# Five early W2 blocks by id ahead of the full W2, and b2's rows spread by GpSimd

## The chip, the cores and the metric

The kernel runs on one core of one Trainium2 chip. The metric is the device time of one execution in microseconds, as the median of several. One execution was also taken by the hardware profiler; it has a span, from the first to the last instruction of the program, and an own time, which holds a little work around the span.

## What is computed

For each of 128 batches there is a block x of 128 tokens by 512 channels and an id between 0 and 8, which picks one of ten languages (W1 512x128, b1, W2 128x512, b2, gamma, beta). Everything is float32.

```python
w1, w2 = W1[ids], W2[ids]
h = relu(einsum('bsh,bha->bsa', x, w1) + b1[ids][:, None, :])
r = x + einsum('bsa,bah->bsh', h, w2) + b2[ids][:, None, :]
normed = (r - mean(r)) * rsqrt(var(r) + 1e-5)
return x + normed * gamma[ids][:, None, :] + beta[ids][:, None, :]
```

## The kernel before

A batch is a tile of 128 tokens by 512 channels. For each one TensorE turns x by four transposes (`transpose_x`, L271), ScalarE copies the result out of PSUM (`copy_xT`, L275), TensorE makes the first product with W1 in four steps (`down`, L294), ScalarE applies relu with b1 (`relu`, L302), and TensorE makes the second product with W2 (`up`, L311). b2 gets into the sum in one of three ways, chosen by batch: TensorE adds it by a small matmul in front of the second product (`b2_by_matmul`, L310), VectorE adds it to the product (`b2_by_vector`, L321), or GpSimd adds it to x beforehand (`add_b2`, L281). VectorE adds x and sums the row (`residual`, L328), ScalarE squares and sums (`square`, L351), and the square root and some short steps give 1/std. VectorE applies mean and gamma (`scale`, L394) and 1/std, and adds it to x + beta (`finish`, L403), which GpSimd has made beforehand in an output buffer (`add_beta`, L288). Two batches share one output buffer and one store (`store`, L407).

The engines work on different batches at one time, and the order on each engine, the SP queue included, is the order of the calls (`keep` chains each instruction to the one before it on its engine). The main loop issues, per turn, the transposes of one batch, the first product of the batch before it, and the second product of the batch two behind.

Before the loop stands an opening written out by hand. It loads the rows of beta, gamma and b2 once (30 rows) and splits them into bf16 parts. Each row that the adds read must stand on all 128 partitions. `spread` does this for one row by a matmul (L229) and a copy on ScalarE (L232); `shuffle_rows` does it for one row by a stream shuffle on VectorE (L247) out of a tile that holds the rows four times (`four_copies`). Rows 0 to 9 are beta, 10 to 19 gamma, 20 to 29 b2. An add takes its row by the id from the whole tile (`beta_b`, `gamma_b`, `b2_b`), so it waits until all ten rows are there. `spin` runs matmuls on ones, whose results nobody reads.

All loads but three small ones go through SP's queue, and each load waits until the eighth before it has landed. x comes by groups of four batches in four buffers (`load_part` for the first twenty batches, `load_x` later). W1 comes in two ways: for the first 17 batches one block of 256 KB by the batch's id into one of seven buffers (`load_first`, L161), and as a whole by four loads of 640 KB (`load_w1`, L103), out of which ScalarE copies one block per batch from batch 17 on (`stage_w1`, L262). W2 comes as a whole, in two loads: three languages, then seven (`load_w2`, L165); the second products read it by the id, so each of them waits for both loads. The order in SP's queue in the opening is this:

```python
load_w2(0, 3); load_first(0); load_first(1); load_part(2, 4); load_first(2); load_first(3)
load_w2(3, L); load_part(4, 6); load_first(4); load_first(5); load_part(6, 8); load_first(6) ...
```

GpSimd starts with some constants and an affine select for the identity, then waits for beta's rows. There are eight output buffers of two batches each.

Of the kernel before, what the change touches and what calls it, by code (L numbers as in the profile page):

```python
# [20 lines left out]
EARLY = 17  # L21
LATE = 17
U = 2


@with_exitstack
def cond_resid_kernel(ctx: ExitStack, tc: tile.TileContext, x, itok, W1, b1, W2, b2, gamma, beta, out):
# [18 lines left out]
    def keep(ins):  # L46

        engine = ins.ins.engine
        if engine in last:
            tc.add_manual_dep(ins.ins, last[engine], behind, reason="kept order")  # L50
        last[engine] = ins.ins.name
        return ins
# [1 line left out]
    const = ctx.enter_context(tc.tile_pool(name="const", bufs=1))  # L54
    xp = ctx.enter_context(tc.tile_pool(name="xp", bufs=4))
    rp = ctx.enter_context(tc.tile_pool(name="rp", bufs=4))
    op = ctx.enter_context(tc.tile_pool(name="op", bufs=8))
    tp = ctx.enter_context(tc.tile_pool(name="tp", bufs=2))
    wp = ctx.enter_context(tc.tile_pool(name="wp", bufs=7))
    st = ctx.enter_context(tc.tile_pool(name="st", bufs=6))  # L60
# [25 lines left out]
    def load_part(lo, hi, engine=nc.sync):  # L86
        dst = xs[lo // G][:, lo % G : lo % G + hi - lo, :]
        keep(engine.dma_start(out=dst, in_=x[lo:hi].rearrange("b s h -> s b h")))  # L88

    warm = const.tile([P, 1], FP, name="warm")  # L90
    keep(nc.vector.memset(warm, 1.0))

# [2 lines left out]
    keep(nc.sync.dma_start(out=rows[L : 2 * L, :], in_=gamma))  # L95
    keep(nc.scalar.dma_start(out=rows[2 * L : 3 * L, :], in_=b2))
    load_part(0, 2)
    keep(nc.scalar.dma_start(out=b1r, in_=b1))
    keep(nc.scalar.activation(warm, warm, AF.Abs_reciprocal_sqrt))

    def load_w1(k):
        keep(
            nc.sync.dma_start(out=w1[:, :, k, :], in_=W1[:, k * P : (k + 1) * P, :].rearrange("l p a -> p l a"))  # L103
        )
# [35 lines left out]
    def lid(b, engine):  # L140
        g = b // G
        if (g, engine) not in lids:
            loads, vals = nc.values_load_multi_w_load_instructions(  # L143
                lang[0:1, g * G : (g + 1) * G],
                engines=[engine],
                min_val=0,
                max_val=L - 1,
                skip_runtime_bounds_check_because="clamped on the chip to 0..L-1 above",
            )
            for ins in loads:  # L150
                keep(ins)
            lids[g, engine] = vals
        return lids[g, engine][b % G]
# [4 lines left out]
    def load_first(b):  # L158
        w1s[b] = wp.tile([P, KC, A], FP, tag="w1s", name=f"w1s_{b}")
        src = W1[bass.ds(lid(b, ET.SP), 1)].rearrange("o (p k) a -> p (o k a)", k=KC)  # L160
        keep(nc.sync.dma_start(out=w1s[b].rearrange("p k a -> p (k a)"), in_=src))  # L161

    def load_w2(lo, hi):
        dst = w2[:, lo * H : hi * H].rearrange("p (l h) -> p l h", l=hi - lo)
        keep(nc.sync.dma_start(out=dst, in_=W2[lo:hi].rearrange("l a h -> a l h")))  # L165

    load_w2(0, 3)
    load_first(0)
    load_first(1)
    load_part(2, 4)  # L170
    load_first(2)
    load_first(3)
    load_w2(3, L)
    xs[1] = xp.tile([P, G, H], FP, tag="x", name="x_1")
    load_part(4, 6)
    load_first(4)
    load_first(5)
    load_part(6, 8)
    load_first(6)
    load_first(7)  # L180
    xs[2] = xp.tile([P, G, H], FP, tag="x", name="x_2")
    load_part(8, 10)
    load_first(8)
    load_first(9)
    load_part(10, 12)
    load_first(10)
    load_first(11)
    xs[3] = xp.tile([P, G, H], FP, tag="x", name="x_3")
    load_part(12, 14)
    load_first(12)  # L190
    load_w1(0)
    load_first(13)
    load_part(14, 16)
    load_first(14)
    load_w1(1)
    load_first(15)
    xs[4] = xp.tile([P, G, H], FP, tag="x", name="x_4")
    load_part(16, 18)
    load_w1(2)
    load_w1(3)  # L200
    load_first(16)
    load_part(18, 20)
# [17 lines left out]

    beta_b = const.tile([P, L * H], FP, name="beta_b")
    gamma_b = const.tile([P, L * H], FP, name="gamma_b")
    b2_b = const.tile([P, L * H], FP, name="b2_b")

    def spread(r, copier):
        t = (beta_b, gamma_b, b2_b)[r // L]
        row = p_y.tile([P, H], FP, tag="y", name=f"row_{r}")
        pick_r = pick[:, r : r + 1].to_broadcast([96, P])
        keep(nc.tensor.matmul(row, lhsT=pick_r, rhs=parts[:96, :], start=True, stop=True))  # L229
        dst = t[:, r % L * H : (r % L + 1) * H]  # L230
        if copier is nc.scalar:
            keep(nc.scalar.copy(dst, row))  # L232
        else:
            keep(nc.vector.tensor_copy(dst, row))

    fours = {}

# [6 lines left out]
    def shuffle_rows(lo, hi):  # L244
        for r in range(lo, hi):
            t = (beta_b, gamma_b, b2_b)[r // L]
            keep(nc.vector.stream_shuffle(t[:, r % L * H : (r % L + 1) * H], fours[0], [r] * 32))  # L247
# [3 lines left out]


    def b2_by_matmul(b):
        return b in (0, 1) or b >= B - 2

    def b2_by_vector(b):
        return b in (2, 3, 9, 13, 17, 21) or 24 <= b < B - 8 and (b % 16 in (1, 6, 11) or b % 32 == 30)

    def stage_w1(b):
        w1s[b] = wp.tile([P, KC, A], FP, tag="w1s", name=f"w1s_{b}")  # L260
# [43 lines left out]
    def up(b):  # L304
        v = lid(b, ET.PE)
        ys[b] = p_y.tile([P, H], FP, tag="y", name=f"py_{b}")
        m = b2_by_matmul(b)
        if m:
            pick_b = pick[:, bass.ds(v + 2 * L, 1)].to_broadcast([96, P])
            keep(nc.tensor.matmul(ys[b], lhsT=pick_b, rhs=parts[:96, :], start=True, stop=False))  # L310
        keep(nc.tensor.matmul(ys[b], lhsT=hT[b], rhs=w2[:, bass.ds(v * H, H)], start=not m, stop=True))  # L311
        del hT[b]

    def col(tiles, b):
# [210 lines left out]
    def spin(n, width):  # L525
        idle = p_s.tile([P, H], FP, tag="s", name="idle")
        for _ in range(n):
            keep(
                nc.tensor.matmul(
                    idle[:, :width], lhsT=ones, rhs=ones[:, 0:1].to_broadcast([P, width]), start=True, stop=True  # L530
                )
            )
# [6 lines left out]

    spin(7, H)  # L540
    four_copies()
    spread(10, nc.scalar)
    spin(1, H)
    x_turn(0)
    transpose_b1()
    spread(11, nc.scalar)
    for n in (0, G):
        lid(n, ET.PE)
    shuffle_rows(0, 10)
    x_turn(1)  # L550
    spread(12, nc.scalar)
    spread(13, nc.scalar)
    down(0)
    relu(0)
    spread(14, nc.scalar)
    x_turn(2)
    spread(15, nc.scalar)
    down(1)
    relu(1)
    spread(16, nc.scalar)  # L560
    spread(17, nc.scalar)
    x_turn(3)
    down(2)
    relu(2)
    spread(18, nc.scalar)
    spread(19, nc.scalar)
    add_beta(0)
    add_beta(1)
    spread(20, nc.scalar)
    spread(21, nc.scalar)  # L570
    down(3)
    relu(3)
    spread(22, nc.scalar)
    add_beta(2)
    add_beta(3)
    shuffle_rows(23, 30)
    up(0)
    up(1)
    x_turn(4)

    turned = 5
    for i in range(3, B - 6):
        b = i - U - 1
        if b == 8 or b > 12 and b % G == 2 and b // G + 3 < NG:
            load_x(5 if b == 8 else b // G + 3)
        up_to = i
        if b <= E:
            if turned <= up_to and on(turned):
                transpose_x(turned)
            add_b2(b + 2)  # L590
            if 4 <= b + 2 <= E:
                add_beta(b + 2)
        for n in range(turned, min(B, up_to) + 1):
            if on(n) and (n > turned or b > E):
                transpose_x(n)
            down(n - 1)
            if on(n):
                copy_xT(n)
            relu(n - 1)
            if on(n + 1) and n + 1 >= FIRST:  # L600
                stage_w1(n + 1)
        turned = max(turned, min(B, up_to) + 1)
        if i - U >= 2 and on(i - U):
            up(i - U)

        g, half = divmod(b, 2)
        p = g - 1
        mine, old = 0 <= p < B // 2, 0 <= p - 1 < B // 2
        if half == 0:
            if on(b):  # L610
                vector_b2(b)
                residual(b)
                square(b)
            if mine:
                scale(2 * p)
                rstd(p, 1)
            if old:
                finish(2 * p - 1)
                store(p - 1)
        else:  # L620
            if on(b):
                vector_b2(b)
            if mine:
                rstd(p, 2)
            if on(b):
                residual(b)
                square(b)
            if mine:
                rstd(p, 3)
                scale(2 * p + 1)  # L630
            if mine:
                finish(2 * p)
        if 0 <= g and b <= E and half == 1:
            scalar_means(g)
            deviation(g)

        for n, engine in ((turned + 2, ET.Activation), (i - U + 3, ET.PE), (b + 1, ET.DVE), (b + 6, ET.Pool)):
            if on(n):
                lid(n, engine)
# [189 lines left out]
```

## Time and profile before

| | us |
|---|---|
| median of 3 runs | 303.18 |
| all runs | 303.14 to 303.38 |
| profiled execution, own time | 303.08 |
| its span | 301.3 |

| engine | busy us | share of the span |
|---|---|---|
| PE (TensorE) | 293.5 | 97% |
| DVE (VectorE) | 294.0 | 98% |
| ACT (ScalarE) | 278.5 | 92% |
| POOL (GpSimd) | 281.0 | 93% |

The granted clock is full over the whole span. The transfers move 78.11 MB. In timeline rows the first figure is the start in us from the span's start, the second the duration in us; SP rows give the time that the issue took on the queue, not the transfer's. PE shows a float32 matmul as two records, so a first product has eight and a second product two. The last figure of a row of DMA issues is the time from issue to landing in us.

### The profile page before, as it was taken

Reading aid. Unit: us, or ns where it says so; the run is one execution under the profiler, and the core shown is the slowest. Engines: PE = TensorE matmul, PEld = TensorE weight load, DVE = VectorE, ACT = ScalarE, POOL = GpSimd, SP = SyncE. Lnnn points to the kernel's source line nnn. Section 1 sums busy time; section 2 is a strip of 40 time slices with the busy share of each in tenths; the row PEclk is TensorE's granted clock in tenths of the full one; section 3 lists DMA queues with packets and bytes.
Section 4 is the critical chain, followed back from the end, with each engine's and each line's share of the span. In section 5 each row is a group of like instructions: output and inputs, shape, how many; then the busy total and the mean of one; then the engine's idle time right before and its main releaser. Section 6 shows DMA issues by size and latency. Waiting matters only on the chain.

```text
span 301.3 us, 7022 instructions
## 1 busy us (share of the span) xinstructions
PE 293.5 (97%) x1827; PEld 219.1 (73%) x1827; DVE 294.0 (98%) x785; ACT 278.5 (92%) x770; POOL 281.0 (93%) x236
## 2 busy tenths in 40 slices
PE   7899999999999999999999999999999999999993
PEld 3758787777777777777777777777777777777761
DVE  6989999999999999999999999999999999999996
ACT  5868789999999999999999999999999999999983
POOL 1299998999999999999999999999999999999982
PEclk9999999999999999999999999999999999999999
DMA  6999999996667776766687666668765767782826
GB/s 234 377 390 367 346 321 396 405 337 209 234 229 256 280 235 197 252 242 233 240 281 250 209 209 246 257 231 281 263 204 196 254 232 253 278 271 79 280 89 228
DMA packets 45353, 78.11 MB, mean 259 GB/s; under 512 B 2137, under 2 KB 9316, under 8 KB 45314
## 3 DMA queue, kind: packets, MB, share of 16 engines
q1 hardware_dynamic: 45254, 77.62, 74.9%
q8 instruction: 15, 0.25, 0.3%
q14 instruction: 24, 0.20, 0.2%
q10 hardware_dynamic: 60, 0.05, 0.1%
HBM read 44.11 MB, written 33.55 MB: 258 GB/s over the span
## 4 chain that ended last, share of the span: by engine, by line
PE 87%; DVE 5%; DMA 3%; issue 2%; SPq 1%; POOL 0%; DVEq 0%; POOLq 0%
PE ph L294 35%; PE py L311 35%; PE pxT L271 18%; DMA w<-in_L_cond_W_dram 3%; DVE py L328 1%; DVE o L488 1%; DVE py L394 1%; SPq L161 1%; DVE n L494 0%; SPq L143 0%; DVE rstd_of L370 0%; SPq L88 0%; DVEq L824 0%; DVE part_of L367 0%; DVE shift L434 0%
## 5 line engine op out<-in xcount | busy, mean ns | idle before, releaser
L288 POOL TENSOR_TENSOR o<-x,beta_b 128x512 f32<-128x512 f32 x121 | 158.4, 1331 | 12.8 <-DVE beta_b L247 11.6
L294 PE MATMUL ph<-xT,w1s 128*128 128x128 f32 x1024 | 135.4, 275 | 0.1
L311 PE MATMUL py<-w,hT 128*128 x256 | 131.5, 595 | 0.6 <-DMA w<-in_L_cond_W_dram 0.6
L294 PEld LDWEIGHTS ph<-xT,w1s 128*128 128x128 f32 x1024 | 124.9, 192 | 1.8 <-issue 0.8
L281 POOL TENSOR_TENSOR r<-x,b_b 128x512 f32<-128x512 f32 x92 | 122.7, 1334 | 0.0
L271 PEld LDWEIGHTS pxT<-ident,x 128*128 128x128 f32 x512 | 65.8, 149 | 66.3 <-issue 49.9
L394 DVE SCALAR_TENSOR_TENSOR py<-py,nmean,gamma_b 128x512 f32<-128x512 f32 x124 | 93.2, 752 | 0.0
L403 DVE SCALAR_TENSOR_TENSOR o<-py,rstd,o 128x512 f32<-128x512 f32 x116 | 86.5, 745 | 0.0
L351 ACT ACTIVATE sq<-py,sum 128x512 f32<-128x512 f32 x124 | 85.8, 692 | 0.2 <-DVE rstd L370 0.2
L275 ACT COPY xT<-pxT 128x512 f32<-128x512 f32 x128 | 74.7, 584 | 5.9 <-PE pxT L271 5.8
L271 PE MATMUL pxT<-ident,x 128*128 128x128 f32 x512 | 77.6, 274 | 0.9 <-ACT gamma_b L232 0.7
L328 DVE SCALAR_TENSOR_TENSOR py<-py,r 128x512 f32<-128x512 f32 x97 | 66.7, 688 | 0.1
L262 ACT COPY w1s<-w 128x512 f32 x108 | 66.2, 613 | 0.0
L302 ACT ACTIVATE hT<-ph,b1T 128x128 f32<-128x128 f32 x128 | 46.9, 367 | 8.6 <-PE ph L294 4.0
L311 PEld LDWEIGHTS py<-w,hT 128*128 128x128 f32 x256 | 39.0, 192 | 2.2 <-DMA w<-in_L_cond_W_dram 1.1
L351 ACT ACTIVATION_READ_ACCUMULATOR sq<-py,sum 128x1 f32 x124 | 25.1, 203 | 0.0
L328 DVE SCALAR_TENSOR_TENSOR py<-py,x 128x512 f32<-128x512 f32 x31 | 21.7, 699 | 0.8 <-PE py L311 0.3
L321 DVE TENSOR_TENSOR py<-py,b_b 128x512 f32<-128x512 f32 x27 | 18.6, 689 | 0.8 <-ACT xT L275 0.6
L361 ACT ACTIVATE root<-ssq,eps 128x2 f32<-128x2 f32 x62 | 16.4, 265 | 0.0
L328 DVE DVE_READ_ACCUMULATOR py<-py,r 128x1 f32 x97 | 13.4, 138 | 0.0
L342 ACT ACTIVATE nmean<-sum 128x2 f32<-128x2 f32 x61 | 12.1, 199 | 0.0
L370 DVE SCALAR_TENSOR_TENSOR rstd<-part,root 128x2 f32<-128x2 f32 x62 | 9.2, 149 | 0.0
(73 smaller groups left out, 104.5 us busy)
## 6 DMA issues: line engine op xcount, KB each, us to landing
out_dram<-o SPq DMA_DIRECT2D x62, 512.0 KB, 3.5
x<-in_x_dram SPq DMA_DIRECT2D x27, 1024.0 KB, 6.5
x<-in_x_dram SPq DMA_DIRECT2D x10, 512.0 KB, 6.0
w1s<-in_L_cond_W_dram SPq DMA_DIRECT2D x20, 256.0 KB, 7.7
w<-in_L_cond_W_dram SPq DMA_DIRECT2D x4, 640.0 KB, 8.4
w<-in_L_cond_W_dram SPq DMA_DIRECT2D x1, 1792.0 KB, 10.2
w<-in_L_cond_W_dram SPq DMA_DIRECT2D x1, 768.0 KB, 5.2
out_dram<-o SPq DMA_DIRECT2D x4, 128.0 KB, 1.7
```

The costliest lines, as they stand in the source:

```text
L262: keep(nc.scalar.copy(w1s[b].rearrange("p k a -> p (k a)"), src))
L271: keep(nc.tensor.transpose(pxs[b][:, k, :], cols, ident))
L275: keep(nc.scalar.copy(xT[b], pxs.pop(b)))
L281: keep(nc.gpsimd.tensor_tensor(rs[b], xb(b), b2_b[:, bass.ds(v * H, H)], ALU.add))
L288: keep(nc.gpsimd.tensor_tensor(os[g][:, j, :], xb(b), beta_b[:, bass.ds(v * H, H)], ALU.add))
L294: nc.tensor.matmul(phs[b], lhsT=w1s[b][:, k, :], rhs=xT[b][:, k, :], start=(k == 0), stop=(k == KC - 1))
L302: keep(nc.scalar.activation(hT[b], phs.pop(b), AF.Relu, bias=b1T[:, bass.ds(lid(b, ET.Activation), 1)]))
L311: keep(nc.tensor.matmul(ys[b], lhsT=hT[b], rhs=w2[:, bass.ds(v * H, H)], start=not m, stop=True))
L328: nc.vector.scalar_tensor_tensor(ys[b], ys[b], 1.0, r, ALU.mult, ALU.add, accum_out=col(sums, b))
L351: nc.scalar.activation(sq, ys[b], AF.Square, bias=col(sums, b), scale=-float(H), accum_out=col(ssqs, b))
L394: nc.vector.scalar_tensor_tensor(ys[b], ys[b], col(nmeans, b), gamma_b[:, bass.ds(v * H, H)], ALU.add, ALU.mult)
L403: nc.vector.scalar_tensor_tensor(o, ys[b], rstds[g][:, j : j + 1], o, ALU.mult, ALU.add)
```

## The change

W2 of batches 0 to 4 is also loaded by id, one block of 256 KB each, into three output buffers (`early_w2`, `load_early`), and their second products read those blocks. The full W2 comes in one load behind the loads of x and W1 for the first eight batches. The ten rows of b2 are loaded once more, as one row of 5120 values on one partition, and GpSimd spreads them over all partitions in two broadcasts of 2560 columns; the b2 rows no longer go through matmuls and shuffles. The built program has, on GpSimd, a switch of its code library in front of the broadcasts and one back behind them, in front of the first add of beta. Output buffers go from eight to nine. Of the twenty rows of beta and gamma eight go by matmul and copy, twelve by shuffle. b2 goes by matmul also for batches 4 and 7, and by VectorE for 2, 6, 9, 17, 19 of the first 24 (before: 2, 3, 9, 13, 17, 21); the rest stays with GpSimd. In the opening the second product of batch 0 comes behind the first product of batch 2. In the queue, x of batches 2 to 9 comes batch by batch, x of batches 16 and 17 ahead of W1 of batch 14, and the loads of the full W1 behind it. The load of x for batches 20 to 23 is issued two turns sooner.

```diff
+SOON = 5
-    op = ctx.enter_context(tc.tile_pool(name="op", bufs=8))
+    op = ctx.enter_context(tc.tile_pool(name="op", bufs=9))
...
     load_part(0, 2)
+    keep(nc.scalar.dma_start(out=b2_b[0:1, :], in_=b2.rearrange("(o l) h -> o (l h)", o=1)))
     keep(nc.scalar.dma_start(out=b1r, in_=b1))
...
+    def early_w2(b):
+        if b // 2 not in soon:
+            soon[b // 2] = op.tile([P, 2, H], FP, tag="o", name=f"soon_{b // 2}")
+        return soon[b // 2][:, b % 2, :]
+
+    def load_early(b):
+        src = W2[bass.ds(lid(b, ET.SP), 1)].rearrange("o a h -> a (o h)")
+        keep(nc.sync.dma_start(out=early_w2(b), in_=src))
...
-    load_w2(0, 3)
     load_first(0)
     load_first(1)
-    load_part(2, 4)
     load_first(2)
+    load_part(2, 3)
     load_first(3)
-    load_w2(3, L)
+    load_early(0)
+    load_part(3, 4)
+    load_early(1)
+    load_first(4)
     xs[1] = xp.tile([P, G, H], FP, tag="x", name="x_1")
-    load_part(4, 6)
-    load_first(4)
+    load_part(4, 5)
+    load_early(2)
+    load_early(3)
     load_first(5)
-    load_part(6, 8)
+    load_early(4)
     load_first(6)
     load_first(7)
+    load_part(5, 6)
+    load_part(6, 7)
+    load_part(7, 8)
+    load_w2(0, 10)
...
     load_part(12, 14)
-    load_first(12)
-    load_w1(0)
+    load_part(14, 16)
     load_first(13)
-    load_part(14, 16)
-    load_first(14)
-    load_w1(1)
-    load_first(15)
     xs[4] = xp.tile([P, G, H], FP, tag="x", name="x_4")
     load_part(16, 18)
+    load_first(14)
+    load_w1(0)
+    load_w1(1)
     load_w1(2)
+    load_first(15)
     load_w1(3)
     load_first(16)
     load_part(18, 20)
...
+    for half in range(2):
+        cols = slice(half * (L // 2) * H, (half + 1) * (L // 2) * H)
+        keep(nc.gpsimd.partition_broadcast(b2_b[:, cols], b2_b[0:1, cols]))
...
-        return b in (0, 1) or b >= B - 2
+        return b in (0, 1, 4, 7) or b >= B - 2
...
-        return b in (2, 3, 9, 13, 17, 21) or 24 <= b < B - 8 and ...
+        return b in (2, 6, 9, 17, 19) or 24 <= b < B - 8 and ...
...
-        keep(nc.tensor.matmul(ys[b], lhsT=hT[b], rhs=w2[:, bass.ds(v * H, H)], start=not m, stop=True))
+        rhs = early_w2(b) if b < SOON else w2[:, bass.ds(v * H, H)]
+        keep(nc.tensor.matmul(ys[b], lhsT=hT[b], rhs=rhs, start=not m, stop=True))
...
-        if b == 8 or b > 12 and b % G == 2 and b // G + 3 < NG:
-            load_x(5 if b == 8 else b // G + 3)
+        if b == 6 or b > 12 and b % G == 2 and b // G + 3 < NG:
+            load_x(5 if b == 6 else b // G + 3)
```

More of the change, by code (lines that the diff above doesn't have):

```diff
@@ L88, in load_part @@
         keep(engine.dma_start(out=dst, in_=x[lo:hi].rearrange("b s h -> s b h")))
+    b2_b = const.tile([P, L * H], FP, name="b2_b")
     warm = const.tile([P, 1], FP, name="warm")
@@ L161, in load_first @@
         keep(nc.sync.dma_start(out=w1s[b].rearrange("p k a -> p (k a)"), in_=src))
+    soon = {}
+    def early_w2(b):
[5 more added lines that the diff above has]
+        keep(nc.sync.dma_start(out=early_w2(b), in_=src))
     def load_w2(lo, hi):
@@ L165, in load_w2 @@
         keep(nc.sync.dma_start(out=dst, in_=W2[lo:hi].rearrange("l a h -> a l h")))
-    load_w2(0, 3)
     load_first(0)
     load_first(1)
-    load_part(2, 4)
     load_first(2)
+    load_part(2, 3)
     load_first(3)
-    load_w2(3, L)
+    load_early(0)
+    load_part(3, 4)
+    load_early(1)
+    load_first(4)
     xs[1] = xp.tile([P, G, H], FP, tag="x", name="x_1")
-    load_part(4, 6)
-    load_first(4)
+    load_part(4, 5)
+    load_early(2)
+    load_early(3)
     load_first(5)
-    load_part(6, 8)
+    load_early(4)
     load_first(6)
     load_first(7)
+    load_part(5, 6)
+    load_part(6, 7)
+    load_part(7, 8)
+    load_w2(0, 10)
     xs[2] = xp.tile([P, G, H], FP, tag="x", name="x_2")
-    load_part(8, 10)
+    load_part(8, 9)
+    load_part(9, 10)
     load_first(8)
@@ L187, in cond_resid_kernel @@
     load_first(11)
+    load_first(12)
     xs[3] = xp.tile([P, G, H], FP, tag="x", name="x_3")
     load_part(12, 14)
-    load_first(12)
-    load_w1(0)
+    load_part(14, 16)
     load_first(13)
-    load_part(14, 16)
-    load_first(14)
-    load_w1(1)
-    load_first(15)
     xs[4] = xp.tile([P, G, H], FP, tag="x", name="x_4")
     load_part(16, 18)
+    load_first(14)
+    load_w1(0)
+    load_w1(1)
     load_w1(2)
+    load_first(15)
     load_w1(3)
@@ L222, in cond_resid_kernel @@
     gamma_b = const.tile([P, L * H], FP, name="gamma_b")
-    b2_b = const.tile([P, L * H], FP, name="b2_b")
     def spread(r, copier):
@@ L253, in b2_by_matmul @@
     def b2_by_matmul(b):
-        return b in (0, 1) or b >= B - 2
+        return b in (0, 1, 4, 7) or b >= B - 2
     def b2_by_vector(b):
-        return b in (2, 3, 9, 13, 17, 21) or 24 <= b < B - 8 and (b % 16 in (1, 6, 11) or b % 32 == 30)
+        return b in (2, 6, 9, 17, 19) or 24 <= b < B - 8 and (b % 16 in (1, 6, 11) or b % 32 == 30)
     def stage_w1(b):
@@ L541, in cond_resid_kernel @@
     four_copies()
-    spread(10, nc.scalar)
-    spin(1, H)
+    spread(17, nc.scalar)
+    shuffle_rows(3, 4)
     x_turn(0)
     transpose_b1()
[L546 to L549, printed above, removed]
+    lid(0, ET.PE)
+    lid(G, ET.PE)
     x_turn(1)
-    spread(12, nc.scalar)
-    spread(13, nc.scalar)
+    shuffle_rows(0, 1)
+    spin(1, H)
+    shuffle_rows(10, 11)
+    shuffle_rows(6, 7)
+    shuffle_rows(16, 17)
+    spread(1, nc.scalar)
     down(0)
     relu(0)
-    spread(14, nc.scalar)
+    shuffle_rows(5, 6)
     x_turn(2)
-    spread(15, nc.scalar)
     down(1)
     relu(1)
-    spread(16, nc.scalar)
-    spread(17, nc.scalar)
+    shuffle_rows(14, 15)
+    shuffle_rows(4, 5)
+    spread(9, nc.scalar)
     x_turn(3)
@@ L564, in cond_resid_kernel @@
     relu(2)
-    spread(18, nc.scalar)
-    spread(19, nc.scalar)
+    up(0)
+    shuffle_rows(2, 3)
+    spread(11, nc.scalar)
+    spread(8, nc.scalar)
+    spread(15, nc.scalar)
+    shuffle_rows(19, 20)
+    shuffle_rows(7, 8)
     add_beta(0)
-    add_beta(1)
-    spread(20, nc.scalar)
-    spread(21, nc.scalar)
     down(3)
     relu(3)
-    spread(22, nc.scalar)
+    add_beta(1)
+    spread(13, nc.scalar)
     add_beta(2)
     add_beta(3)
-    shuffle_rows(23, 30)
-    up(0)
+    x_turn(4)
+    shuffle_rows(18, 19)
     up(1)
-    x_turn(4)
+    spread(12, nc.scalar)
     turned = 5
```

## The prediction

> **What bounds the kernel now.** I read the page first (shares, then the chain), then PE's rows, and then the queue of loads, because the change is made in the first 50 us.
>
> ```profile
> PE 293.5 (97%) x1827; PEld 219.1 (73%) x1827; DVE 294.0 (98%) x785; ACT 278.5 (92%) x770; POOL 281.0 (93%) x236
> PE 87%; DVE 5%; DMA 3%; issue 2%; SPq 1%; POOL 0%; DVEq 0%; POOLq 0%
> ```
>
> All four engines are nearly full, but the chain that ended last is PE's. Its order of time begins with a load, and from there PE's rows follow each other without a gap:
>
> ```profile
> 6.22 10.17 DMA w<-in_L_cond_W_dram
> ...
> 23.53 1.02 PE L311 MATMUL py<-w,hT 128*128 x2
> ...
> 25.75 1.02 PE L311 MATMUL py<-w,hT 128*128 x2
> ```
>
> The second part of the full W2 is issued at 6.22 and lands at 16.39; batch 0's second product starts behind it. 23.53 and 25.75 are the second products of batches 4 and 5: 2.22 us a batch, PE's own work. So the time is the moment at which PE reaches its steady pace, plus a fixed rest. Whatever delays PE before about batch 17 is paid once, in full; whatever lets it start sooner is gained only if no later operand is late.
>
> The operands come through one queue. Four stretches of the trace (length, then busy time of PE, PEld, DVE, ACT, POOL, then clock, DMA share, GB/s):
>
> ```profile
> 4.00:16.40 12.40, 10.28 (x66) 7.57 (x65) 11.37 (x35) 10.32 (x23) 3.30 (x3) 1.00 1.03 379
> 16.40:28.00 11.60, 11.57 (x66) 8.30 (x67) 10.43 (x29) 8.11 (x23) 11.60 (x11) 1.00 1.05 386
> 28.00:48.00 20.00, 20.00 (x129) 15.69 (x128) 19.82 (x51) 16.21 (x47) 18.83 (x16) 1.00 1.11 340
> 48.00:100.00 52.00, 52.00 (x332) 39.30 (x332) 51.94 (x138) 50.80 (x142) 52.00 (x43) 1.00 0.81 287
> ```
>
> The DMA share is over 1 up to 48 us and 0.81 behind it. In the opening the queue has no room: a byte put in front of a load delays it by the byte's own time.
>
> **The queue, in blocks.** I count in blocks of 256 KB (one batch of x, one W1 of one language, one W2 of one language) in the order of issue. Issue rows and, below each, the last figure of its DMA row (us to landing):
>
> ```profile
> 3.75 0.91 SPq L161 DMA_DIRECT2D w1s<-in_L_cond_W_dram  x2
> w1s<-in_L_cond_W_dram SPq DMA_DIRECT2D x1, 256.0 KB, 4.1
> ...
> 16.52 1.68 SPq L161 DMA_DIRECT2D w1s<-in_L_cond_W_dram  x2
> w1s<-in_L_cond_W_dram SPq DMA_DIRECT2D x1, 256.0 KB, 8.5
> ...
> 37.63 2.82 SPq L161 DMA_DIRECT2D w1s<-in_L_cond_W_dram  x1
> w1s<-in_L_cond_W_dram SPq DMA_DIRECT2D x1, 256.0 KB, 7.1
> ```
>
> Batch 0's W1 is the 6th block (two of x, three of W2 before it) and lands at 3.75 + 4.1 = 7.85. The end of W2 is the 18th, at 16.39: 0.71 us a block. Batch 8's W1 is the 29th, at 16.52 + 8.5 = 25.0: 0.78 a block. Batch 16's W1 is the 55th, at 37.63 + 7.1 = 44.7; the four loads of the full W1 (10 blocks) lie between, the last as block 54, at about 44.0. At 386 GB/s a block takes 0.68 us.
>
> **What the change puts in the queue.** The full W2 (10 blocks) stays, and five blocks (W2 of batches 0 to 4 by id) are added in front of it. W2 now ends as block 31 (8 of x, 8 of W1, 5 + 10 of W2), the full W1 as block 59, batch 16's W1 as block 60. One more cost: the 3 blocks of W2 that filled the queue while SP waited for the ids are gone from there. Batch 0's W1 is still issued at 3.75, with two blocks in front of it whose load was issued at 1.52 and landed 3.4 later:
>
> ```profile
> 1.52 0.41 SPq L88 DMA_DIRECT2D x<-in_x_dram  x1
> x<-in_x_dram SPq DMA_DIRECT2D x1, 512.0 KB, 3.4
> ```
>
> 3.4 less two blocks (1.4) is a delay of 2.0, so block 3 lands at 3.75 + 2.0 + 0.7 = 6.4, where a queue without a hole would have it at 4.9 + 0.7 = 5.6. The hole is worth 0 to 0.8 us; I take 0.7.
>
> W2 ends at 25.0 + 2 x 0.68 + 0.7 = **27.1** (26.4 without the hole). Batch 5's second product is the first that needs it, and it stood at 25.75: PE is 0.7 to 1.3 us later than before, whatever it gained earlier. Eight smaller blocks are in flight behind W2, so the queue does not run dry while SP waits for W2 to land before it issues batch 12's W1.
>
> Then batch 16's W1 and the full W1. Their readers stood here:
>
> ```profile
> 47.03 1.06 PE L294 MATMUL ph<-xT,w1s 128*128 128x128 f32 x8
> ...
> 46.20 0.61 ACT L262 COPY w1s<-w 128x512 f32 x1
> ```
>
> Batch 16's W1 lands 5 x 0.68 + 0.7 = 4.1 us later, at 48.8, and its product stood at 47.03: +1.8. The full W1 ends at 44.0 + 4.1 = 48.1, and ScalarE's first copy out of it stood at 46.20: +1.9, with the square of batch 13 and the copy of batch 17's x queued behind it on ScalarE; PE waits for that copy. These waits overlap the one at batch 5 and do not add to it: the largest counts, with some 0.2 for the coupling of the two. **Sum: +2.0 us**, bounds +1.1 (no hole) and +2.8 (a second hole as large).
>
> **What is gained and hidden.** Each of these costs or brings nothing, because PE stands waiting for W2 until 27.1 or for W1 until 48.8. If that cover were gone they would count.
>
> ```profile
> 13.50 1.03 PE L229 MATMUL row<-parts,pick 96*128 96x512 bf16 x4
> 16.43 1.12 PE L311 MATMUL py<-w,hT 128*128 x2 [0.58 <-DMA w<-in_L_cond_W_dram]
> 10.04 0.72 PE L271 MATMUL pxT<-ident,x 128*128 128x128 f32 x4 [0.71 <-ACT gamma_b L232]
> 1.70 0.35 ACTq L98 DMA_DIRECT2D b1r<-in_L_cond_b_dram  x1
> L247 DVE STREAM_SHUFFLE b_b<-four x7: 791/795/801, 12.9 to 16.8; 128x512 f32<-128x512 f32 x7
> ```
>
> - Spreads by matmul go from 13 to 8: (1.03 - 0.38) / 3 = 0.22 each, so 1.1 us off PE, and five copies off ScalarE. b2 by matmul for batches 4 and 7: +0.22 each.
> - The waits of 0.58 and 0.71 go. Batch 0's second product can start when its own W2 block is there (block 8, near 10 us). PE alone would reach batch 5 at 25.75 - 1.1 + 0.2 - 1.3 + 0.3 = 23.9, and then waits some 3 us.
> - The load of the b2 row on ScalarE's queue delays its table load and the split rows by 0.3.
> - Shuffles on VectorE go from 17 to 12 at (16.8 - 12.9) / 6 = 0.65: 3.3 us off its opening. b2 on VectorE goes from six of the first 24 batches to five. VectorE follows PE, so neither is seen.
> - The first x of group 4 moves in front of three W1 loads on SP and waits for batch 3's readers, done by then. Loading x 20 to 23 is issued one store sooner.
> - Output buffers: three of nine hold early W2 at first; the tenth pair (batch 18) waits for the first store where the ninth (batch 16) waited 1.17. GpSimd has that much in hand (below).
>
> **GpSimd.** It idles to 13.10 and then adds without a pause, 4.98 / 4 = 1.24 us each:
>
> ```profile
> 0.89 0.20 POOL masks.py:197 MEMSET ident<- 128x128 f32 x1
> 1.03 0.10 POOL L111 MEMSET eps<- 128x1 f32 x1
> 1.17 0.29 POOL masks.py:199 TENSOR_SCALAR_AFFINE_SELECT ident<-ident 128x128 f32<-128x128 f32 x1
> 13.10 4.98 POOL L288 TENSOR_TENSOR o<-x,beta_b 128x512 f32<-128x512 f32 x4 [11.64 <-DVE beta_b L247]
> masks.py:199 POOLq MODIFY_POOL_CONFIG  x2: 11/11/11, 1.1 to 1.1; - x2
> ```
>
> Added: two broadcasts of 128x2560, and a switch of GpSimd's code before them and back before the first add. No row shows a broadcast. The add (1.24 for 512 columns) gives 6.2 us each; the select less a memset of one column, (0.29 - 0.10) / 127 a column, gives 3.8; the memset alone, (0.20 - 0.10) / 127, gives 2.0. I take 3, between the last two: it writes as the memset does, and reads one row. A switch costs nothing in the one row that has it (0.01 us, the select follows at once). So the adds could begin between 1.5 + 4.0 = 5.5 and 1.5 + 12.4 = 13.9, and beta's rows hold them to 13.1 anyway (shuffles end near 13).
>
> How late may they be? b2 of batch 5 is the 7th add (four of beta, b2 of 3, beta of 4): 8.7 us after the start. VectorE wants it when batch 5's product ends, 27.1 + 1.0 = 28.1. So up to a start at **19.4** nothing is lost; each us beyond costs one, since later on 25 of 32 batches have both adds, 57 x 1.24 / 32 = 2.2 us a batch, which cannot catch up. Later there is more in hand:
>
> ```profile
> 68.53 1.28 POOL L281 TENSOR_TENSOR r<-x,b_b 128x512 f32<-128x512 f32 x1
> 73.16 0.70 DVE L328 SCALAR_TENSOR_TENSOR py<-py,r 128x512 f32<-128x512 f32 x1
> ```
>
> Batch 26 is among the tightest: b2 ready at 69.81, used at 73.16, and GpSimd has one add less by then.
>
> The Trainium skill speaks against this part: GPSIMD Engine Reference, 2.1 Instruction dispatch, says the first call to a freshly loaded kernel pays about 6 us for loading code, with no instruction that shows it. No run here shows such a first call; the select's row shows none. By the page two switches put the first add at 1.5 + 6 + 6 + 6 = 19.5, on the edge of the cover.
>
> **Rivals.**
> 1. *GpSimd begins too late* (chance 0.20). If the switches take long, or the broadcast has the add's pace, the first add comes at 21 to 23. Price: 1.6 to 3.6 more, **307.7**. It decides from 19.4 on. For it: two switches to code that this kernel never called; against it: the 0.01 us of the row. The page just named gives this case with broadcasts over 3 us.
> 2. *W2 lands in time* (0.12, faster). If blocks land at 0.65 us instead of 0.71 to 0.78, and those behind W2 at 0.70, W2 ends at 6.4 + 28 x 0.65 = 24.6 and batch 16's W1 at 24.6 + 29 x 0.70 = 44.9; PE's own 23.9 is then covered up to 24.6: 25.75 - 24.6 = 1.2 us gained, **301.9**. It decides where W2 ends before 25.7 and batch 16's W1 before 47.0. Against it: 379 to 386 GB/s with the share over 1 in both stretches. The Trainium skill (DMA: Bandwidth & Descriptors, Specifications) names a ceiling of 435 GB/s, an estimated 0.60 us a block, and would give this case; the rows stay 11% under it.
> 3. *No change* (0.08). The queue's own stops hide the blocks: from block 18 to 29 it took 25.0 - 16.39 = 8.6 us where 11 x 0.68 is 7.5. If that stop of 1.1 falls elsewhere, and no hole opens, 2.0 - 1.1 - 0.7 = +0.2 is left: **303.3**. It decides where batch 16's W1 lands by 47.3.
>
> **How the numbers follow.** The profiled execution took 303.08 with a span of 301.3; the median of three is 303.18. 303.1 + 2.0 = **305.1** (0.60 for this case). The range reaches down to the no-change case and up to 1's middle: **303.2 to 308.2**; the forecast's own bounds are 304.2 to 305.9. Within 0.2% (0.6 us, about what a measurement can tell) is rival 3: same 0.08; faster 0.12; slower 0.60 + 0.20 = 0.80.
>
> **What would show it.** Right: the chain of waits begins with the load of W2 ending at 26.4 to 27.2; PE waits about 3 us before batch 5's second product; ScalarE's first copy out of W1 and batch 16's first product wait for loads near 48; then 2.2 us a batch to the same tail. Wrong: PE without a wait at batch 5, W2 before 25.7, or VectorE waiting for GpSimd's sums past batch 5.

## The result, and the profile after

The changed kernel takes 311.91 us in the median (four runs, 311.05 to 313.71), the kernel before 303.28 beside it: a ratio of 1.030 with an interval of 1.028 to 1.032, slower by 8.6 us. The forecast was 305.1 with a range to 308.2; the sign was right, the size was not. The profiled execution is the longest of the four, 313.71 with a span of 311.9, and is compared with before's own profiled execution (303.08, 301.3): 10.6 us more.

The page after: engine shares, the chain that ended last, and the granted clock in 40 slices of 7.8 us.

```profile
PE 296.8 (95%) x1824; PEld 222.1 (71%) x1824; DVE 290.6 (93%) x774; ACT 276.7 (89%) x765; POOL 285.2 (91%) x237
...
PEclk9897599999999999999999999999999999999999
...
PE 88%; DVE 5%; issue 3%; POOL 2%; ACT 1%; DMA 1%; ACTq 0%; DVEq 0%; POOLq 0%
```

Read by shares, little has happened: every busy time is within a few us of before's. What is new is a clock of 0.8, 0.7 and 0.5 in the second, fourth and fifth slice (a 9 stands for 90% or more), where it was full, and the chain, which has no long DMA piece any more but one of POOL. GpSimd's timeline says why (start, duration, then in brackets the idle time before):

```profile
1.41 0.29 POOL masks.py:199 TENSOR_SCALAR_AFFINE_SELECT ident<-ident 128x128 f32<-128x128 f32 x1 [0.29 <-POOL eps L114]
8.42 5.48 POOL L259 PARTITION_BROADCAST b_b<-b_b  x2 [6.73 <-issue]
24.77 4.91 POOL L313 TENSOR_TENSOR o<-x,beta_b 128x512 f32<-128x512 f32 x4 [10.87 <-issue]
29.65 1.25 POOL L306 TENSOR_TENSOR r<-x,b_b 128x512 f32<-128x512 f32 x1
```

The two broadcasts take 5.48 together. Around them GpSimd stands idle for 6.73 and 10.87 us, both "issue": no semaphore is late. The row of b2 had landed at 4.55, beta's last row was written by 16.5. The first add starts at 24.77 where it stood at 13.10 before. The load of the full W2, issued at 15.72, has fifteen of its sixteen parts landed by 27.16 and the last at 28.71 (by the updates of its semaphore in the trace), so W2 is not what comes last. The chain of waits around PE's stop:

```profile
22.33 0.91 PE ph L319 x8
23.23 0.02 issue
23.26 0.38 ACT hT L327
23.64 1.13 issue
24.77 4.70 POOL o L313 x4
...
29.85 1.05 POOL r L306
...
30.93 0.07 DVE py L354
...
32.28 0.76 DVE o L429
33.04 0.04 issue
33.09 2.08 PE py L337 x2
```

The fifth add is b2 of batch 3 (29.65 to 30.90). VectorE's sum of batch 3 waits for it, `finish` of batch 0 stands behind that sum on VectorE (32.28), and only `finish` gives back the PSUM buffer that batch 5's second product needs. That product starts at 33.09; before it stood at 25.75: 7.3 us. The rest of the 10.6 follows at once. PE's rows behind it:

```profile
33.09 2.08 PE L337 MATMUL py<-w,hT 128*128 x2 [7.42 <-DVE o L429]
34.95 1.06 PE L296 MATMUL pxT<-ident,x 128*128 128x128 f32 x4
35.81 1.92 PE L319 MATMUL ph<-xT,w1s 128*128 128x128 f32 x8
37.52 1.30 PE L337 MATMUL py<-w,hT 128*128 x2
...
40.24 1.02 PE L337 MATMUL py<-w,hT 128*128 x2
```

and four stretches of 4 us (length, busy time of PE, PEld, DVE, ACT, POOL, then granted clock, DMA share, GB/s):

```profile
24.00:28.00 4.00, 1.66 (x13) 1.33 (x11) 0.00 (x0) 0.00 (x0) 3.23 (x3) 0.98 1.05 387
28.00:32.00 4.00, 0.00 (x0) 0.00 (x0) 1.07 (x4) 0.28 (x1) 4.00 (x4) 0.50 1.05 388
32.00:36.00 4.00, 2.91 (x7) 1.78 (x8) 3.81 (x12) 2.36 (x8) 4.00 (x5) 0.50 1.04 383
36.00:40.00 4.00, 4.00 (x23) 3.39 (x22) 2.49 (x6) 2.51 (x7) 4.00 (x4) 0.74 0.63 192
```

PE idled from 25.67 to 33.09; the clock falls to 0.50 two us into that and stays there until 38.1, so a second product takes 2.08 instead of 1.02. Batch 7's second product starts at 40.24, against 25.75 + 2 x 2.22 = 30.19 before: 10.05 later. From there to batch 120 the distance stays at 10.1. The Trainium skill (TensorE: Matmul & The Clock Gate, What's actually happening) describes a clock that is halved after an idle window of about 3.4 us. The trace agrees in part: the halved stretch of 10.2 us is three times that long, but it began 2.2 us after PE's last matmul, sooner than a whole idle window.

The 0.8 of the second slice is another stretch: from 7.4 to 10.8 us the clock is 0.50 too, while PE was at work again after short pauses. Batch 0's first product took 1.91 us there, where it took 1.13 in the kernel before.

### The profile page after: what moved, and what is told of

Read it like the earlier page. It is cut to its first block, busy times and chain, and to the rows that moved or that the text cites. A ratio compares the mean times of both kernels' runs of the same rounds, so it can differ in the third digit from the quotient of the medians.

```text
span 311.9 us, 7027 instructions
## 1 busy us (share of the span) xinstructions
PE 296.8 (95%) x1824; PEld 222.1 (71%) x1824; DVE 290.6 (93%) x774; ACT 276.7 (89%) x765; POOL 285.2 (91%) x237
## 4 chain that ended last, share of the span: by engine, by line
PE 88%; DVE 5%; issue 3%; POOL 2%; ACT 1%; DMA 1%; ACTq 0%; DVEq 0%; POOLq 0%
PE ph L319 35%; PE py L337 34%; PE pxT L296 18%; POOL o L313 2%; DVE py L354 1%; DVE o L514 1%; DVE py L420 1%; PE row L250 1%; DMA rows<-in_L_cond_b_dram 1%; DVE n L520 0%; POOL r L306 0%; DVE o L429 0%; PE py L335 0%; ACT parts L233 0%; ACT xT L300 0%
## 5 line engine op out<-in xcount | busy, mean ns | idle before, releaser
L313 POOL TENSOR_TENSOR o<-x,beta_b 128x512 f32<-128x512 f32 x121 | 152.2, 1266 | 10.9 <-issue 10.9
L319 PE MATMUL ph<-xT,w1s 128*128 128x128 f32 x1024 | 137.2, 277 | 0.0
L337 PE MATMUL py<-w,hT 128*128 x246 | 127.7, 601 | 7.4 <-DVE o L429 7.4
L319 PEld LDWEIGHTS ph<-xT,w1s 128*128 128x128 f32 x1024 | 126.6, 194 | 1.7 <-ACT hT L327 0.7
L306 POOL TENSOR_TENSOR r<-x,b_b 128x512 f32<-128x512 f32 x91 | 115.2, 1265 | 0.0
L296 PE MATMUL pxT<-ident,x 128*128 128x128 f32 x512 | 78.5, 276 | 0.6 <-ACT xT L300 0.5
L327 ACT ACTIVATE hT<-ph,b1T 128x128 f32<-128x128 f32 x128 | 46.9, 367 | 10.6 <-PE ph L319 6.4
L337 PEld LDWEIGHTS py<-w,hT 128*128 128x128 f32 x246 | 37.9, 194 | 8.4 <-DVE o L429 7.6
L347 DVE TENSOR_TENSOR py<-py,b_b 128x512 f32<-128x512 f32 x26 | 17.9, 690 | 1.8 <-PE py L337 1.5
L387 ACT ACTIVATE root<-ssq,eps 128x2 f32<-128x2 f32 x62 | 16.5, 266 | 0.0
L368 ACT ACTIVATE nmean<-sum 128x2 f32<-128x2 f32 x61 | 12.1, 199 | 0.0
L259 POOL PARTITION_BROADCAST b_b<-b_b x2 | 5.5, 2800 | 6.7 <-issue 6.7
```

The source lines that it names most:

```text
L296: keep(nc.tensor.transpose(pxs[b][:, k, :], cols, ident))
L306: keep(nc.gpsimd.tensor_tensor(rs[b], xb(b), b2_b[:, bass.ds(v * H, H)], ALU.add))
L313: keep(nc.gpsimd.tensor_tensor(os[g][:, j, :], xb(b), beta_b[:, bass.ds(v * H, H)], ALU.add))
L319: nc.tensor.matmul(phs[b], lhsT=w1s[b][:, k, :], rhs=xT[b][:, k, :], start=(k == 0), stop=(k == KC - 1))
L327: keep(nc.scalar.activation(hT[b], phs.pop(b), AF.Relu, bias=b1T[:, bass.ds(lid(b, ET.Activation), 1)]))
L337: keep(nc.tensor.matmul(ys[b], lhsT=hT[b], rhs=rhs, start=not m, stop=True))
```

## Experiments

Times are medians of four runs unless said otherwise; each was taken beside the kernel before, whose medians were 302.98 to 303.08. "The distance" is how much later a batch's second product starts than in before's trace.

**1. No broadcast.** The changed kernel, with b2's rows made as before.

```diff
-    keep(nc.scalar.dma_start(out=b2_b[0:1, :], in_=b2.rearrange("(o l) h -> o (l h)", o=1)))
...
-    for half in range(2):
-        cols = slice(half * (L // 2) * H, (half + 1) * (L // 2) * H)
-        keep(nc.gpsimd.partition_broadcast(b2_b[:, cols], b2_b[0:1, cols]))
...
     shuffle_rows(18, 19)
+    shuffle_rows(23, 30)
     up(1)
     spread(12, nc.scalar)
+    spread(20, nc.scalar)
+    spread(21, nc.scalar)
+    spread(22, nc.scalar)
```

> The changed kernel with the ten b2 rows made as before (three spreads, seven shuffles) and no broadcast on GpSimd. Theory (the two switches of GpSimd's code hold the first add to 24.8 us, and the later W2 costs something of its own): the first add starts near 16.5, when beta's last row is there; batch 5's second product waits for the full W2 alone, at 28.7 where before it stood at 25.75, so about +3.0, and up to 2.5 more if the granted clock falls during that wait: 306 to 308.5. Rival A (the lateness of GpSimd is the whole loss, the early W2 pays): 302 to 303.5. Rival B (GpSimd's switches are not the cause): still about 312.

Measured: 305.66, ratio 1.008 (1.007 to 1.010). GpSimd, then PE:

```profile
17.30 4.97 POOL L308 TENSOR_TENSOR o<-x,beta_b 128x512 f32<-128x512 f32 x4 [15.83 <-ACT beta_b L252]
```

```profile
25.47 1.02 PE L332 MATMUL py<-soon,hT 128*128 128x512 f32 x2
...
27.69 1.07 PE L332 MATMUL py<-w,hT 128*128 x2
```

About 6 of the 8.6 us lost go with the broadcast (311.9 - 305.7), and the rest stays. The theory holds but for its lower edge, which it misses by 0.3: W2 landed at 27.54, not 28.7, and PE reached batch 5 only 0.15 later and without a wait, because it was 1.6 late at batch 2 already. The thirteen spreads (eight in the changed kernel) are not the reason: experiment 7 has the same thirteen, and its batch 2 stands 1.9 sooner. The difference is the pace of PE's matmuls up to about 12 us. Batch 0's first and batch 2's second product, here and then in experiment 7:

```profile
9.10 1.91 PE L314 MATMUL ph<-xT,w1s 128*128 128x128 f32 x8
20.57 1.12 PE L332 MATMUL py<-soon,hT 128*128 128x512 f32 x2
...
7.54 1.05 PE L317 MATMUL ph<-xT,w1s 128*128 128x128 f32 x8
18.66 1.13 PE L335 MATMUL py<-soon,hT 128*128 128x512 f32 x2
```

The record gives the clock as 1.00 in both openings, although the same product took almost twice as long here; why is open. Behind 14 us the pace is the usual one.

**2. The broadcast alone**, put into the kernel before.

```diff
+    keep(nc.scalar.dma_start(out=b2_b[0:1, :], in_=b2.rearrange("(o l) h -> o (l h)", o=1)))
...
+    for half in range(2):
+        cols = slice(half * (L // 2) * H, (half + 1) * (L // 2) * H)
+        keep(nc.gpsimd.partition_broadcast(b2_b[:, cols], b2_b[0:1, cols]))
...
-    spread(20, nc.scalar)
-    spread(21, nc.scalar)
...
-    spread(22, nc.scalar)
...
-    shuffle_rows(23, 30)
```

> The kernel before with one part of the change: b2's rows by two broadcasts on GpSimd instead of three spreads and seven shuffles; loads and their order as before. Theory: the first add moves from 13.1 to about 24.8, 11.7 us; GpSimd adds without a pause afterwards, and its smallest lead before was 3.3 us (batch 26), so 8.3 are paid by then: about 311.4, with PE waiting for GpSimd's sums in the first 26 batches. Rival (the loss comes from the later W2, the broadcast is hidden as forecast): under 304.5.

Measured: 314.42, ratio 1.038 (1.035 to 1.040): worse than the whole change. GpSimd:

```profile
10.99 5.48 POOL L239 PARTITION_BROADCAST b_b<-b_b  x2 [9.29 <-issue]
25.44 4.94 POOL L293 TENSOR_TENSOR o<-x,beta_b 128x512 f32<-128x512 f32 x4 [8.97 <-DVE py L399]
```

The switch out takes 9.29 here, where three blocks of W2 fill the queue from the start, and 8.97 back. The first add came 0.6 later than expected, the time is 3.0 over. The distance is 5.8 at batch 6 and 8.9 at batch 8 (the clock is 0.5 from 33.2 to 40.0, which the estimate left out), stays there, and grows to 10.6 in the tail, where GpSimd's lateness is paid once more (experiment 5).

**3. The loads alone**, put into the kernel before: the early W2 blocks, the new order of loads, nine output buffers; no broadcast, opening and choice of batches as before.

> The kernel before with one part of the change: its loads (W2 of batches 0 to 4 by id, the full W2 behind them, the new order) and the nine output buffers; the opening, the rows of b2 and the choice of batches as before. Theory (what the prediction said of the queue): GpSimd's first add stays at 13.1; the full W2 lands at 27.1 to 27.6, batch 5's second product, which stood at 25.75, starts behind it, and batch 16's W1 and the full W1 come some 4 us later: 305.0 to 305.6. Rival A (the queue hides the five blocks): 302.9 to 303.4. Rival B (PE's early start is kept): under 302.5.

Measured: 307.09, ratio 1.014 (1.012 to 1.016); the profiled execution is the shortest of the four, 306.13. GpSimd, then PE:

```profile
14.16 4.99 POOL L308 TENSOR_TENSOR o<-x,beta_b 128x512 f32<-128x512 f32 x4 [12.70 <-DVE beta_b L267]
```

```profile
24.49 1.06 PE L314 MATMUL ph<-xT,w1s 128*128 128x128 f32 x8
28.32 1.10 PE L332 MATMUL py<-w,hT 128*128 x2 [2.77 <-DMA w<-in_L_cond_W_dram]
```

GpSimd's first add comes at 14.16 and not at 13.1, but it is not what batch 5 waits for. This is the forecast's mechanism with nothing in its way: batch 5 waits 2.77 for the full W2 and starts 2.57 later than before; batch 15 adds 0.35, and it stays at 3.0. The size is 0.5 to 1 over what was expected in the profiled execution and 1.5 to 2 in the median: fifteen parts of W2 are there by 26.79, the sixteenth at 28.18. Why the other three runs were 1 us longer than the profiled one is open.

**4. What a switch costs elsewhere.** The kernel before with a broadcast of 8 columns ahead of the sums of batches 42 and 82 (one run).

```diff
+    tiny = const.tile([P, 8], FP, name="tiny")
+    nc.gpsimd.memset(tiny, 1.0)
...
+            if b in (40, 80):
+                keep(nc.gpsimd.partition_broadcast(tiny, tiny[0:1, :]))
             add_b2(b + 2)
```

> The kernel before with a broadcast of one row of 8 columns on GpSimd ahead of batch 42's and batch 82's sums, its result used by nothing: a switch there and back in the steady stretch, where the DMA share is 0.72. Theory 1 (a switch costs the same wherever it stands): the adds stop for about 6.7 us before the small broadcast and 10.9 behind it, at both places; less GpSimd's lead of 3 to 5 us that is some 13 us of PE's time each, and more for the clock: 328 to 334. Theory 2 (the 10.9 in the changed kernel is code loaded against a full queue): 6 to 7 us each way here, 19 or less in all: 316 to 324. Rival (only the first switch loads code, later ones find it there): the second place costs nothing, 309 to 314.

Measured: 330.14. GpSimd at both places:

```profile
108.99 0.28 POOL L593 PARTITION_BROADCAST tiny<-tiny  x1 [5.63 <-issue]
117.52 1.25 POOL L283 TENSOR_TENSOR r<-x,b_b 128x512 f32<-128x512 f32 x1 [8.25 <-issue]
...
211.02 0.28 POOL L593 PARTITION_BROADCAST tiny<-tiny  x1 [5.97 <-issue]
218.31 1.25 POOL L283 TENSOR_TENSOR r<-x,b_b 128x512 f32<-128x512 f32 x1 [7.01 <-issue]
```

The broadcast of 8 columns takes 0.28, and the switches around it 13.9 and 13.0: 13 to 14 in all against 17.6 in the changed kernel, nearer to theory 2, though the time fell into theory 1's range, because PE lost 12.4 and 12.1 at the two places (the clock was 0.5 for 10.2 us behind each) and 2.4 more in the tail. The second trip costs nearly what the first did, so the rival falls.

**5. PE kept at work in its wait.** The changed kernel with batch 6's first product computed nine times over.

```diff
-        for k in range(KC):
+        for k in [*range(KC)] * (9 if b == 6 else 1):
```

> The changed kernel with batch 6's first product computed nine times over in place of once, the last result used: PE then works through most of its wait from 25.7 to 33.1 instead of idling. Theory (of the 8.7 us lost, some 2.7 are the halved clock that follows the idle stretch: batch 5's second product took 2.08 where 1.02 is usual): the clock stays at 1.00, 309.0 to 309.8. Rival (GpSimd sets the pace up to the end of the opening, the clock is hidden behind it): about 312, or more if the repeated products come in the way.

Measured: 311.73, the same as the changed kernel within its spread. The clock did stay full, and PE won by it:

```profile
25.50 8.20 PE L319 MATMUL ph<-xT,w1s 128*128 128x128 f32 x72
33.63 1.13 PE L337 MATMUL py<-w,hT 128*128 x2
...
35.95 1.02 PE L337 MATMUL py<-w,hT 128*128 x2
...
38.39 1.02 PE L337 MATMUL py<-w,hT 128*128 x2
```

Batch 7 stands at 38.39 against 40.24 in the changed kernel, 1.85 sooner, although GpSimd's first add came 0.5 later (25.27). At batch 120 1.7 of it is left, at the last batch 0.8. The chain that ended last, in this kernel's page and then in its tail (283 to 300 us):

```profile
PE 68%; DVE 10%; POOL 9%; issue 9%; POOLq 1%; ACT 1%; DMA 1%; DVEq 0%; ACTq 0%
```

```profile
by line: issue 29.7%; POOL o L449 22.4%; POOL o L313 14.8%; POOL r L453 14.7%; POOL r L306 7.3%; DVE o L514 4.8%; DVE py L420 2.9%; DVE py L354 2.3%; DVE part L391 0.9%; DVE part L393 0.9%; DVE nmean L361 0.9%; DVE shift L460 0.7%; DVEq L42
```

In the tail the chain now runs through GpSimd's adds. GpSimd's start sets two limits: PE's stop at batch 5, and the last adds. The rival was right on the time: most of what PE gains, the tail takes back, and the medians differ by 0.2. The size is less sure than that. In the two profiled executions 0.8 of the 1.85 is left at the end, and the first add's 0.5, which is no doing of the edit, is part of what was lost; what would be left with the same start of GpSimd is not shown.

**6. The switches without the large broadcasts, first try.** Experiment 1 with a broadcast of 8 columns out of a tile of ones in the opening.

> The kernel of the first experiment (the changed kernel, b2's rows made as before) with a broadcast of one row of 8 columns on GpSimd in the opening, its result used by nothing: the two switches of code without the 5.5 us of the large broadcasts. Theory (the switches cost 6.7 to 9.3 and 9.0 to 11.0 us in the opening; from the first add to the end of the run it took 288.4 there, 305.66 - 17.30): first add at 18 to 21, time 306.4 to 309.4, likeliest 307.9. Rival (the large broadcast is the cost, a small one brings no switch worth the name): 305.7.

Measured: 313.28. This did not test what it should: the small broadcast came ahead of the identity's select on GpSimd, the select waited for the switch (8.32 instead of 1.17), and with it the split rows and all PE work, so PE's first matmul on the rows came at 11.75 instead of 4.78. It shows that a switch delays whatever stands behind it on GpSimd, and all that waits for that. Its switch out is of use for another question:

```profile
8.18 0.28 POOL L258 PARTITION_BROADCAST tiny<-tiny  x1 [7.02 <-issue]
```

No load moved from 5 to 11 us, and the switch took 7.02 all the same. In the changed kernel and experiments 5, 7 and 8 it took 6.5 to 7.1, with a mean DMA share of 0.73 to 0.79 over it.

**7. The same behind the identity.**

```diff
+    tiny = const.tile([P, 8], FP, name="tiny")
+    keep(nc.gpsimd.partition_broadcast(tiny, ident[0:1, 0:8]))
```

> The kernel of the first experiment (the changed kernel, b2's rows made as before) with a small broadcast (one row of 8 columns of the identity, its result used by nothing) on GpSimd right behind the identity mask, so that only GpSimd's queue has it: two switches of code without the 5.5 us of the large broadcasts. Theory (the switches are what holds the adds; 6.7 to 7.0 out, 9.0 to 11.0 back): the small broadcast at 8.2 to 8.7, first add at 17.5 to 20, against 17.3 without; 305.7 to 308.5, likeliest 307. Rival 1 (the switch back takes as long as the time until the next add allows, no longer): first add at 17.3, 305.7. Rival 2 (the broadcast's length counts in the switch back): 312.

Measured: 306.18, ratio 1.011 (1.009 to 1.013). GpSimd, then PE:

```profile
8.19 0.28 POOL L257 PARTITION_BROADCAST tiny<-ident  x1 [6.49 <-issue]
18.61 4.95 POOL L311 TENSOR_TENSOR o<-x,beta_b 128x512 f32<-128x512 f32 x4 [10.14 <-ACT b_b L252]
```

```profile
27.47 1.10 PE L335 MATMUL py<-w,hT 128*128 x2 [1.53 <-DMA w<-in_L_cond_W_dram]
```

The switch out takes 6.49 although this broadcast reads nothing that is loaded, the switch back 10.14. The first add is 1.3 later than in experiment 1, so rival 1 falls, and at 306.18 so does rival 2. The time is 0.5 longer (305.66 to 306.81), the low side of the expectation: at 18.6 GpSimd is still early enough, and W2 is what batch 5 waits for. (The releaser named in the second row had finished before; the gap begins at the small broadcast's end.)

**8. Loads held back.** The changed kernel with all loads from x of batch 4 on kept until GpSimd's first add has written (one run).

```diff
     load_early(1)
     load_first(4)
+    def later_loads():
+        hold = const.tile([1, 8], FP, name="hold")
+        keep(nc.sync.dma_start(out=hold, in_=os[0][0:1, 0, 0:8]))
...
     add_beta(0)
+    later_loads()
```

> The changed kernel with all loads from x of batch 4 on held until GpSimd's first add has written (a small copy out of that add's tile stands ahead of them on SP's queue), so that the queue is empty from about 14 us on, while GpSimd switches back. Its time is not the point, it starves the opening. Theory 1 (the switch back takes 9 to 11 us in the opening because its code comes through the loaded queue; with the queue empty it took 7.0 to 8.3 in the steady stretch): first add at 21 to 22.3 instead of 24.8. Theory 2 (the length is the switch's own): first add at 24.3 to 25.

Measured: 319.96. GpSimd, then two stretches (the columns as above):

```profile
8.46 5.48 POOL L262 PARTITION_BROADCAST b_b<-b_b  x2 [6.77 <-issue]
20.69 3.69 POOL L316 TENSOR_TENSOR o<-x,beta_b 128x512 f32<-128x512 f32 x3 [6.75 <-issue]
```

```profile
12.00:14.00 2.00, 2.00 (x18) 1.93 (x17) 2.00 (x6) 1.46 (x5) 1.94 (x1) 1.00 0.12 46
14.00:16.00 2.00, 2.00 (x12) 1.16 (x11) 0.76 (x2) 1.07 (x3) 0.00 (x0) 1.00 0.00 0
```

With the queue empty from 14 us on, the switch back takes 6.75, the same as the switch out, where it took 10.87 against a full queue. The first add, at 20.69, lies 0.3 below theory 1's range and far from theory 2's: without the loads 4.1 of the 10.87 are gone. The two switches back in experiment 4 fit this, 8.25 at a mean DMA share of 0.37 and 7.01 at 0.14. But it is one run, PE and VectorE stood still behind 17 us too, and no row shows the code moving: that the loads are in its way is likely, how is not shown.

**9. Another opening.** Experiment 1 with beta's ten rows shuffled first and b2's rows last.

> The changed kernel without broadcast, as in the first experiment, with the opening put in another order: beta's ten rows are shuffled first, so that GpSimd can start at 13.1 instead of 17.3, and the rows of b2 come last. Theory (the full W2 at 27.1 to 27.6 is the limit): 304.8 to 305.6, no better than the first experiment's 305.66. Rival (GpSimd's start at 17.3 was that experiment's limit): 13.1 + 288.4 = 301.5, or up to 303 with PE's own work.

Measured: 305.94, ratio 1.010 (1.008 to 1.012). GpSimd, then PE:

```profile
13.67 4.99 POOL L308 TENSOR_TENSOR o<-x,beta_b 128x512 f32<-128x512 f32 x4 [12.21 <-DVE beta_b L267]
```

```profile
28.16 1.02 PE L332 MATMUL py<-w,hT 128*128 x2
```

The first add starts at 13.67, 3.6 sooner than in experiment 1, and nothing is gained; batch 5 stands at 28.16, 2.4 later than before. So GpSimd's start was not experiment 1's limit. W2 had landed at 26.95, PE came to it later still: here too batch 0's first product took 1.91, as in experiment 1, and PE's own opening and W2 end within about 1 us of each other.

None of the variants reached 303.

## Why the prediction was right or wrong

**The bound** was read rightly: a delay of PE in the opening is paid once and kept. The distance is 10.05 at batch 7 and 10.1 at batch 120.

**The queue** was right in kind, and in the profiled executions within 1 us in size. W2's end, 27.1, was met by fifteen of its sixteen parts (27.16 in the changed kernel; 26.8 in experiment 3), the last part came 1.4 to 1.6 later, which the blocks did not show. By itself this costs 3.0 in experiment 3's profiled execution, where +2.0 with bounds to +2.8 was worked out, and 4.1 in its median, beyond the bounds; batch 16's W1 and the full W1 added 0.35 to it, not their own 1.8, as "the largest counts" said. Experiments 1, 3, 7 and 9, all without the broadcast of b2, lie at 305.7 to 307.1, against a forecast of 305.1.

**GpSimd is the step that failed**: "a switch costs nothing in the one row that has it". In the sum both switches stood at nothing; they take 6.73 and 10.87, 17.6 together. The row of the affine select, it seems, was of a configuration whose code was in place already; that is inferred from the price of every switch to the broadcast and back in these runs. The broadcasts were sized well, 2.8 each where 3 was taken. So the adds began at 24.77, outside the stated 5.5 to 13.9, and rival 1 decided the case, past its own 21 to 23. The Trainium skill (GPSIMD Engine Reference, 2.1 Instruction dispatch) gave about 6 us for a first call and was set aside on a row that did not bear on it; by it, as the prediction worked out, the first add would have come at 19.5. The traces agree with the page within 1.1 us for the switches out (5.6 to 7.1, but 9.3 in experiment 2) and for the switch back with the queue empty (6.75 in experiment 8), not for the switches back in the opening with the queue full (9.0 to 11.0).

**The threshold** of 19.4 was about right, by another path than the one given. The prediction followed b2 of batch 5 to VectorE at 28.1; what came first was b2 of batch 3, the fifth add, through `finish` of batch 0 to the PSUM buffer of batch 5. From the first add to PE that is 33.09 - 24.77 = 8.3 us, so with W2 at 28.7 a start up to 20.4 costs nothing; with the forecast's 27.1 it would have been 18.8. At 18.6 (experiment 7) it cost nothing that W2 did not.

**What was not in the sum:** the halved clock after the stop, 2.7 us of PE's distance in the profiled execution (7.34 at batch 5, 10.05 at batch 7). Experiment 5 shows that most of it is not paid on top, since the tail waits for GpSimd as well; how much is left is open there.

**What was hidden** stayed hidden: five spreads fewer, the early second product of batch 0 (14.13 against 16.43) and the shorter shuffles brought PE to batch 4 at 23.28, 0.25 sooner than before, and then it waited. The gain itself was put too high: PE alone was to reach batch 5 at 23.9, and was through with the work ahead of it at 25.67. The halved clock from 7.4 to 10.8 us, which the prediction did not have, can account for up to 1.7 of this (an estimate, half of that stretch).

**The range.** Its upper end, 308.2, is called the middle of rival 1; by the prediction's own sum that middle is 307.7, and the rival's price of up to 3.6 ends at 308.7.

## What to carry to other kernels

A custom operation on an engine with loadable code is costed with the switch in front of it and the one behind it; a row that shows no gap may be one that needed no load. Before placing such an operation, look at what its engine is due to do next, follow the first few of those results through the buffers they free, and count the code load against a queue that may be full. When a loaded block is moved ahead in a saturated queue, the time is decided by what then ends last, and an early start that meets that load is worth nothing.

## What the runs showed of the hardware

A switch of GpSimd's code between the adds and a broadcast took 5.6 to 7.1 us outward in seven of eight cases, with a mean DMA share of 0.29 to 0.79 over it, and 9.3 in experiment 2, with 0.94. The switch back took 6.75 with the queue empty, 7.0 and 8.3 in the steady stretch, and 9.0 to 11.0 against the loads of the opening. It was paid each time, also on the second trip. A broadcast of 2560 columns to 128 partitions took 2.80, one of 8 columns 0.28. A stop of PE of 7.4 us was followed by a halved clock for 10.2 us, one of 3.75 (experiment 2) by 6.8 us of it, one of 2.8 by none. A load of 2.5 MB had its last part land 1.4 to 1.6 us behind the other fifteen in the changed kernel and experiment 3.
